# Where layer 3 gets its tiles from: first tile early, last tile from SBUF, next pair's first input made in layer 3

## Chip, cores and metric

The kernel runs on one core of a Trainium2 chip. The metric is device time in microseconds (us). The program computes four convolution layers on 16 images of 192 channels and 64x64 pixels in float32.

## What is computed

Every layer normalises its input in groups of six channels and adds its result to it. Layer 0 is a small per-channel network (a likelihood), layer 1 a convolution over five shifts, layer 2 a selective scan in four directions, layer 3 a depthwise convolution with a 1x1 mix, batch normalisation over all images and a clip. The reference, cut to layers 2 and 3:

```python
# layer 2: for each of 4 directions, over L = 4096 positions
dA = exp(d * A); h = dA * h + (d * u) * B_t; y = sum_n h * C_t      # 16 states n
x = x + ss2d(gn(x))
# layer 3
y = dw(x, w3) + dw(x, w5) + dw(x, wh) + dw(x, wv)     # 3x3, 5x5, 1x7, 7x1 depthwise
z = einsum('oc,bchw->bohw', pw, y)
zn = (z - mean(z)) * rsqrt(var(z) + 1e-5)             # over all images
x = x + clip(gamma * zn + beta, 0, 6)                 # input of dw is gn(x)
```

## The kernel before

Two images make a pair: 384 channels, which are three tiles (`NT`) of 128 partitions and `L` = 4096 columns. The eight pairs go one after the other. For the first pair, `front` (layers 0 and 1, the projections of layer 2) runs by itself; for each later pair it is woven, as a generator, into the `scans` of the pair before. So a pair is `scans(i)`, which also carries `front(i + 1)`, and then `layer3(i)`.

**scans.** For each tile j, direction k (in the order 1, 3, 0, 2) and chunk of 1024 columns there are 16 steps, one for each state n, 768 in all. A step is: `product` (DVE: pbt = du * B, out of PSUM), `scan` (DVE: the recurrence into h; ACT keeps the last column as `state`; POOL multiplies h by cb, the C row, and every fourth step starts a DMA that adds two h), `decay` (ACT: dA for a later step), `spread` (PE: B into PSUM), and `add_up` four steps late (PE: sums h over n into `ysum`; at n = 15 ACT copies it to X or Xt). `step_rest` makes delta and du for the next chunk out of `xn`, the normalised input tile, which `load_xn` and `norm_xn` bring in for each tile. When a tile is done, `finish(j)` adds Xt, transposed, to X in four pieces, takes statistics for layer 3 into `st3`, and stores X to `x3_d` in DRAM. For the last tile these adds are on DVE and nothing is left to run beside them.

**layer3.** It loads the three tiles of `x3_d` into `xp`, with three pixels of zero border, makes 21 diagonal 128x128 matrices on POOL (`diag`, a weight tap of seven for each tile), does the group norm on all three tiles' statistics (`group_norm`), and normalises each tile in place on DVE. Then for c in four pieces of 16 rows and for each tile j: eight taps go as ACT multiplies and POOL adds into `l3_g`; seven taps go as matmuls with `diag` into PSUM `l3_p`, to which PE adds `l3_g`; the last 14 taps go on DVE, one after the other, through `l3_p` into `l3_y`. After the three tiles PE mixes channels with `pw` into `zp`, ACT copies to z, DVE takes statistics, and SP stores z. At the end, when all pairs are done, z and x3 are read back, scaled, clipped and added.

**Order.** The tile framework lists the instructions of each engine in a fixed order at build time, by its own estimate of when each is ready. Instructions of `scans` are marked to stay in the order in which they were written; those of `layer3` are not, and may be put between them. A tile pool opened after others were closed takes their place in SBUF, in the order of opening, and waits for them. In `scans` the order is X, Xt, xn, dt, xc (16, 16, 16, 2 and 4 KB a partition), then bp, delta, du (20 KB in two buffers each), h (8 of 4 KB), dA (3), cb (4), then `front`'s pools; in `layer3` it is the small statistics (under 1 KB), xp (57 KB), pw and diag (14 KB), then l3_g, l3_m, l3_y and z (52 KB).

Line 64 in the profile is the helper through which all instructions of `scans` and a woven `front` go; line 319 is `normalise`.

Of the kernel before, what the change touches and what calls it, by code (L numbers as in the profile page):

```python
# [11 lines left out]
F32 = mybir.dt.float32  # L12
BF16 = mybir.dt.bfloat16
AF = mybir.ActivationFunctionType
ALU = mybir.AluOpType
# [7 lines left out]
P = 128  # L23
C = 192
NT = 3
HW = 64
L = HW * HW
BLOCKS = [(0, 0), (1, 0), (0, 1), (1, 1), (2, 1), (1, 2), (2, 2)]
INTO = [[(n, ji) for n, (ji, jo) in enumerate(BLOCKS) if jo == j] for j in range(NT)]
# [19 lines left out]
TAPS = [(3, 0), (3, 6), (0, 3), (6, 3)] + [(y, x) for y in range(1, 6) for x in range(1, 6)]  # L49
PE_TAPS = 7  # L50
# [54 lines left out]
def conv_preact_kernel(ctx: ExitStack, tc: tile.TileContext, a: dict):  # L105
    nc = tc.nc
    x_in = a["x"]
    out = a["out"]
    npair = x_in.shape[0]

    def row_tiles(ap):
        return ap.rearrange("(j p) l -> p j l", p=P)

    dram = ctx.enter_context(tc.tile_pool(name="dram", bufs=1, space=DRAM))
    x1_d = dram.tile([NT * P, L], F32, name="x1_d")
    x3_d = dram.tile([npair, NT * P, L], F32, name="x3_d")
    z_d = dram.tile([npair, NT * P, L], F32, name="z_d")
    zstat_d = dram.tile([npair, P, NT * 2], F32, name="zstat_d")
    wm_d = dram.tile([P, NG, P + GR], F32, name="wm_d")
    wt_d = dram.tile([GR, NG, 2 * P], F32, name="wt_d")  # L120

    const = ctx.enter_context(tc.tile_pool(name="const", bufs=1))
    ident = const.tile([P, P], F32, name="ident")
# [16 lines left out]
    def load(name, shape, pool=const):  # L140
        t = pool.tile(shape, F32, name="t_" + name, tag="t_" + name)
        nc.sync.dma_start(out=t, in_=a[name])
        return t
# [57 lines left out]
    with tc.tile_pool(name="prep", bufs=1) as prep, tc.tile_pool(  # L201
# [83 lines left out]
        for part, w in (  # L285
            (wc[:, :, 2:5, 2:5], w3x3),
            (wc[:, :, 3, :], w1x7),
            (wc[:, :, :, 3], w7x1),
        ):
            nc.vector.tensor_tensor(part, part, w, ALU.add)  # L290

# [14 lines left out]
            self.rstd = const.tile([P, NT], F32, name=f"rstd{n}")  # L308

    sets = [Made(n) for n in range(2)]  # L310

    def image(ap):
        return ap.rearrange("p (h w) -> p h w", w=HW)
# [4 lines left out]
    def normalise(eng, o, v, gm, rstd, j):  # L318
        eng.tensor_scalar(o, v, gm[:, j : j + 1], rstd[:, j : j + 1], ALU.subtract, ALU.mult)
# [14 lines left out]
                which = self._turn = (self._turn + 1) % self._many  # L334
            return self._pool.tile([P, 512], F32, name=name, tag=f"ps{which}")

    def group_norm(E, st, stat, ps, gm, rstd):

        mv = stat.tile([P, NT, 2], F32, name="mv", tag="mv")
        mean = stat.tile([P, NT], F32, name="mean", tag="mean")  # L340
        d2 = stat.tile([P, NT], F32, name="d2", tag="d2")
        half = stat.tile([P, NT], F32, name="half", tag="half")
        E.dve.memset(half, -0.5)
        for j in range(NT):
            E.dve.bn_aggr(mv[:, j, :], st[:, j, :, :].rearrange("p c s -> p (c s)"))
        E.dve.tensor_copy(mean, mv[:, :, 0])

        def mean_of(src):
            s = ps("gn_sum")
            for jo in range(NT):  # L350
                for n, (b, ji) in enumerate(INTO[jo]):
                    E.pe.matmul(
                        s[:, jo : jo + 1],
                        grp[:, b, :],
                        src[:, ji : ji + 1],
                        start=(n == 0),
                        stop=(n == len(INTO[jo]) - 1),
                    )
                yield
            return s[:, :NT]  # L360

        s = yield from mean_of(mean)
        E.dve.tensor_scalar(gm, s, 1.0 / 6.0, None, ALU.mult)
        E.dve.tensor_tensor(d2, mean, gm, ALU.subtract)
        E.dve.tensor_tensor(d2, d2, d2, ALU.mult)
        E.dve.tensor_tensor(d2, d2, mv[:, :, 1], ALU.add)
        s = yield from mean_of(d2)
        E.dve.tensor_scalar(d2, s, 1.0 / 6.0, 1e-5, ALU.mult, ALU.add)
        E.gps.tensor_tensor(rstd, d2, half, ALU.pow)
# [409 lines left out]
                yield  # L779


    def scans(i, o, st3, nxt):

        E = _Engines(tc, True)
        with ExitStack() as es:
# [11 lines left out]
            py = pool("l2_py", 1, space=PSUM)  # L797
            ps = Banks(pool("l2_ps", 1, space=PSUM), 2)

            X = one.tile([P, L], F32, name="X")  # L800
            Xt = one.tile([P, L], F32, name="Xt")

            todo = []
# [31 lines left out]

            def load_xn(j):
                if j < NT:
                    xns[j] = one.tile([P, L], F32, name="xn")
                    E.sp.dma_start(out=xns[j], in_=row_tiles(o.x2)[:, j, :])

            def norm_xn(j):
                if j < NT:
                    normalise(E.dve, xns[j], xns[j], o.gm, o.rstd, j)
# [119 lines left out]
            def finish(j):  # L963

                for c in range(4):
                    x = X[:, 1024 * c : 1024 * c + 1024]
                    eng = E.gps if j < NT - 1 else E.dve
                    eng.tensor_tensor(
                        image(x), image(x), columns(Xt)[:, 16 * c : 16 * c + 16, :], ALU.add
                    )  # L970
                    yield
                    yield

                    def stats(c=c):
                        for h in range(2 * c, 2 * c + 2):
                            E.dve.bn_stats(st3[:, j, h, :], X[:, 512 * h : 512 * h + 512])

                    E.later(stats)
                yield
                E.sp.dma_start(out=row_tiles(x3_d[i])[:, j, :], in_=X)  # L980

            load_xn(0)
            load_dt(0)
            load_bp(0)
            norm_xn(0)
            for _ in step_rest(0):
                pass
            load_dt(1)
# [6 lines left out]
            kind = None  # L995
            fin = iter(())
            gstep = iter(())
            for s in range(total):
                t, n = divmod(s, N)
                j, k, at, first = todo[t]  # L1000
# [18 lines left out]
                    norm_xn(j + 1)  # L1019
                if n > 4:  # L1020
                    next(fin, None)

                if n == 3:
                    add_up(s - LATE)
# [21 lines left out]
            for g in (finish(NT - 1), fr):  # L1046
                for _ in g:
                    E.between()
            E.between()

    def layer3(i, st3):
        E = _Engines(tc, False)
        with tc.tile_pool(name="l3s", bufs=1) as stat, tc.tile_pool(name="l3x", bufs=1) as xk, tc.tile_pool(
            name="l3w", bufs=1
        ) as w_, tc.tile_pool(name="l3", bufs=2) as wk, tc.tile_pool(
            name="l3_pt", bufs=2, space=PSUM
        ) as pt, tc.tile_pool(name="l3_pz", bufs=4, space=PSUM) as pz:
            S = HW + 6
            xp = xk.tile([P, NT, S, S], F32, name="xp")
            inside = slice(3, 3 + HW)  # L1060
            for j in range(NT):
                nc.sync.dma_start(
                    out=xp[:, j, inside, inside], in_=image(row_tiles(x3_d[i])[:, j, :])
                )
            pw = load("pw", [P, len(BLOCKS), P], w_)
            diag = w_.tile([P, NT, PE_TAPS, P], F32, name="diag")
            for edge in (slice(0, 3), slice(3 + HW, S)):
                nc.gpsimd.memset(xp[:, :, edge, :], 0.0)
                for j in range(NT):
                    nc.gpsimd.memset(xp[:, j, inside, edge], 0.0)  # L1070
            for j in range(NT):
                for t, (ty, tx) in enumerate(TAPS[:PE_TAPS]):
                    nc.gpsimd.tensor_scalar(
                        diag[:, j, t, :], ident, wc[:, j, ty, tx : tx + 1], None, ALU.mult
                    )
            gm = stat.tile([P, NT], F32, name="gm")
            rstd = stat.tile([P, NT], F32, name="rstd")
            banks = lambda name: pz.tile([P, 512], F32, name=name, tag="ps")
            for _ in group_norm(E, st3, stat, banks, gm, rstd):
                pass  # L1080
            for j in range(NT):
                v = xp[:, j, inside, inside]
                normalise(nc.vector, v, v, gm, rstd, j)
            zst = stat.tile([P, NT, 8, 6], F32, name="zst")
            def window(j, c, rows, tap):
                return xp[:, j, c + tap[0] : c + tap[0] + rows, tap[1] : tap[1] + HW]

            def factor(j, tap):
                return wc[:, j, tap[0], tap[1] : tap[1] + 1]

            own = PE_TAPS + GP_TAPS
            for c in range(4):
                ys = []
                for j in range(NT):

# [58 lines left out]
            for j in range(NT):  # L1154
                nc.vector.bn_aggr(zmv[:, j, :], zst[:, j, :, :].rearrange("p c s -> p (c s)"))
            nc.sync.dma_start(out=zstat_d[i], in_=zmv.rearrange("p j s -> p (j s)"))

    def pair(i, q, more):

        with tc.tile_pool(name="st3", bufs=1) as p3:  # L1160
            st3 = p3.tile([P, NT, 8, 6], F32, name="st3")
            scans(i, sets[q], st3, None if more is None else (more, sets[1 - q]))
            layer3(i, st3)

    with tc.tile_pool(name="f_ps", bufs=1, space=PSUM) as ps:
        for _ in front(0, sets[0], _Engines(tc, False), Banks(ps, 8), True):
            pass
    for i in range(npair):
        pair(i, i % 2, i + 1 if i + 1 < npair else None)


    with tc.tile_pool(name="fin", bufs=1) as fin, tc.tile_pool(
# [164 lines left out]
```

## Time and profile before

| | |
|---|---|
| median of three runs | 28266.48 us (28245.82 to 28275.6) |
| profiled execution | 28295.17 us, span of its instructions 28293.1 us |
| busy share | DVE 86%, PE 83%, POOL 73%, ACT 57% |
| DVE, costliest | scans of h 10811.0 + 3509.0 us, products 7441.2 us, taps of layer 3 1589.7 us |
| POOL, costliest | h*cb 14853.6 us, adds of layer 3 1614.3 us |
| first pair: first product, last scan ended | 1212.9, 4207.9 us |
| first pair: layer 3, first tap to last statistics | 4254.3 to 4555.1 us |
| second pair: first product | 4572.6 us |

The page of a profile counts, for each engine, the time in which it executed something; matmuls overlap one another, so PE's share says least. A share over the whole span is a mean over stages with different limits. The stage between the end of one pair's scans and the start of the next pair's is therefore read from the timeline, instruction by instruction, with, in brackets, how long the engine stood idle before and what ended that.

### The profile page before, as it was taken

The page shows a single profiled execution, that of the slowest core. Times are in us where ns is not written, and L with a number is a line of the kernel's source. Part 1 is how long each engine was busy: PE and PEld are TensorE (multiplying, and loading weights), DVE is VectorE, ACT ScalarE, POOL GpSimd, SP SyncE. Part 2 cuts the span into 40 slices and gives each one's busy share as a digit, 9 for nine tenths or more (in the row PEclk, how much of TensorE's full clock was granted, in tenths as well). Part 3 has the DMA queues.
Part 4 walks back from the last instruction along what each step waited for, and adds up shares of the span by engine and source line. Part 5 has one row for each costly group of instructions (what it writes and reads, how often), then busy time and mean ns, then how long its engine had stood idle before and what let it go on. Part 6 is the DMA issues. An engine that isn't in the chain of part 4 may idle for free. (4 is left out here: it accounts for less than half of the span.)

```text
span 28293.1 us, 208020 instructions
## 1 busy us (share of the span) xinstructions
PE 23483.5 (83%) x57140; PEld 9639.0 (34%) x57140; DVE 24223.9 (86%) x15397; ACT 16092.7 (57%) x23037; POOL 20787.2 (73%) x10440
## 2 busy tenths in 40 slices
PE   8799977999689986999779997799968998766663
PEld 4343323333233332333324332333323333222221
DVE  0399988998889988999989998899988998899994
ACT  7377445774467643775547744577446764344433
POOL 2388876887768876788768887688777887677772
PEclk9899988999899998999889998899989999888886
DMA  4479864897568973888748986489756897367765
GB/s 101 133 219 220 213 199 139 220 218 211 159 180 222 218 215 116 219 218 220 210 125 218 219 215 198 136 220 219 213 162 176 220 219 212 115 189 191 191 182 232
DMA packets 2008001, 5447.99 MB, mean 193 GB/s; under 512 B 550393, under 2 KB 550617, under 8 KB 1989425
## 3 DMA queue, kind: packets, MB, share of 16 engines
q1 hardware_dynamic: 1782192, 4578.95, 56.1%
q0 software_dynamic: 221184, 805.40, 14.9%
q10 hardware_dynamic: 3456, 50.33, 0.4%
q8 instruction: 455, 7.45, 0.1%
q14 instruction: 714, 5.84, 0.1%
HBM read 3896.19 MB, written 329.51 MB: 149 GB/s over the span
## 5 line engine op out<-in xcount | busy, mean ns | idle before, releaser
L64 POOL TENSOR_TENSOR h<-h,cb 128x1024 f32<-128x1024 f32 x6144 | 14853.6, 2465 | 4470.5 <-ACT state L64 3854.4
L64 DVE TENSOR_TENSOR_SCAN h<-dA,state,pbt 128x1024 f32<-128x1024 f32 x4608 | 10811.0, 2346 | 659.1 <-ACT dA L64 97.5
L64 PE MATMUL ysum<-h,ident 128*128 128x512 f32 x18432 | 9459.7, 638 | 191.6 <-DMA h<-h 144.7
L64 DVE TENSOR_TENSOR pbt<-du,pbt 128x1024 f32<-128x1024 f32 x6144 | 7441.2, 1211 | 852.4 <-PE pbt L64 812.1
L64 ACT ACTIVATE dA<-delta,t_alog 128x1024 f32<-128x1024 f32 x6144 | 7034.8, 1146 | 6.6
L64 PEld LDWEIGHTS ysum<-h,ident 128*128 128x128 f32 x18432 | 3780.8, 206 | 4474.2 <-issue 3926.6
L64 ACT COPY state<-h 128x1 f32<-128x1 f32 x6144 | 1141.0, 186 | 6533.9 <-DVE h L64 6508.4
L64 PE MATMUL pbt<-bp,pick 96*128 96x512 bf16 x8192 | 2729.3, 418 | 1942.8 <-DVE h L64 1931.8
L64 DVE TENSOR_TENSOR_SCAN h<-dA,pbt 128x1024 f32<-128x1024 f32 x1536 | 3509.0, 2285 | 181.5 <-DVE pbt L64 30.8
L64 PE MATMUL p<-t,wts 96*128 96x512 f32 x5376 | 2783.4, 618 | 164.0 <-ACT t L64 163.0
L64 PE MATMUL p<-m,wms 128*96 128x512 f32 (+1 forms) x5376 | 2720.3, 609 | 12.0 <-ACT lu L64 12.0
L64 ACT ACTIVATE t<-p,bias 96x512 f32<-96x512 f32 x2688 | 1803.6, 678 | 1162.8 <-PE p L64 1151.6
L64 PEld LDWEIGHTS <-pick 96*128 96x128 bf16 x8192 | 715.6, 102 | 4759.1 <-DVE h L64 2927.7
L1104 POOL TENSOR_TENSOR l_g<-l_g,l_m 128x1024 f32<-128x1024 f32 x672 | 1614.3, 2404 | 454.4 <-ACT l_g L1100 349.0
L64 PE MATMUL l_p<-l_xp,w1s 128*128 128x512 f32 x3920 | 1868.7, 609 | 0.0
L1127 DVE SCALAR_TENSOR_TENSOR l_p<-xp,wc,l_p 128x1024 f32<-128x1024 f32 x1248 | 1589.7, 1287 | 266.6 <-PE l_p L1121 235.8
L64 PE MATMUL pbt<-bp,pick_mix 96*128 96x512 bf16 x4096 | 1302.3, 401 | 569.8 <-DVE h L64 564.9
L64 POOL DMA_DIRECT2D h<-h x1536 | 1354.3, 882 | 495.1 <-POOL h L64 429.8
L1109 PE MATMUL l_p<-xp,diag 128*128 128x512 f32 x2688 | 1293.2, 641 | 331.9 <-DVE l_y L1127 281.2
L64 PEld LDWEIGHTS p<-t,wts 96*128 96x128 f32 x5376 | 1032.6, 195 | 1335.9 <-issue 903.1
L64 ACT ACT_TABLE_LOAD x1104 | 1416.4, 1283 | 19.3
L64 POOL TENSOR_TENSOR du<-delta,xn 128x1024 f32<-128x1024 f32 x384 | 1039.1, 2706 | 452.4 <-ACT delta L64 452.4
(219 smaller groups left out, 17710.1 us busy)
## 6 DMA issues: line engine op xcount, KB each, us to landing
cb<-cp_d SPq DMA_DIRECT2D x2048, 512.0 KB
cb<-c_d SPq DMA_DIRECT2D x2048, 512.0 KB
h<-h POOLq DMA_DIRECT2D x1536, 512.0 KB, 7.0
cb<-cp_d SPq DMA_DIRECT2D x2048, 256.0 KB
cb<-c_d SPq DMA_DIRECT2D x2048, 256.0 KB
m<-l_xn SPq DMA_DIRECT2D x3072, 128.0 KB
bp<-bp_d SPq DMA_DIRECT2D x384, 192.0 KB
f0x<-in_x SPq DMA_DIRECT2D x96, 512.0 KB
```

Source lines behind the costliest of these rows:

```text
L64: return self._tc.keep_in_program_order(call(*args, **kw))
L1104: nc.gpsimd.tensor_tensor(g, g, m, ALU.add)
L1109: nc.tensor.matmul(ps[:, cs], diag[:, j, t, :], window(j, 16 * c + 8 * h, 8, tap), start=(t == 0), stop=False,)
L1127: nc.vector.scalar_tensor_tensor(image(y if tap is TAPS[-1] else ps), window(j, 16 * c, 16, tap), factor(j, tap), image(ps), ALU.mult, ALU ...
```

## The change

Five things are changed together.

1. The 21 diagonal matrices are made once, in the preparation, and stored to `diag_d`; each `layer3` loads them.
2. `X` and `xn` move into a pool `over` that stays open. The last tile's sum isn't read back from `x3_d`: layer 3 normalises it out of X, and its store stands behind the loads of layer 3.
3. `group_norm` can be done for some tiles. A first one over tiles 0 and 1 (`gn0`) runs in the last 11 steps of the scans; it gives the mean and the scale of tile 0, whose groups end in tile 1. Layer 3 normalises tile 0 with these, in four pieces, before the group norm of all three.
4. `xp` becomes three tiles, in a pool opened last in layer 3, placed in the order 2, 0, 1.
5. The next pair's first `xn` is loaded and normalised in `layer3`, written at c = 2; the first pair's after the first `front`. `scans` begins without it.

```diff
+    diag_d = dram.tile([P, NT, PE_TAPS, P], F32, name="diag_d")
...
+        for j in range(NT):
+            diag = prep.tile([P, PE_TAPS, P], F32, name="diag", tag="diag", bufs=2)
+            for t, (ty, tx) in enumerate(TAPS[:PE_TAPS]):
+                nc.gpsimd.tensor_scalar(
+                    diag[:, t, :], ident, wc[:, j, ty, tx : tx + 1], None, ALU.mult
+                )
+            nc.sync.dma_start(out=diag_d[:, j, :, :], in_=diag)
...
+    over = ctx.enter_context(tc.tile_pool(name="over", bufs=1))
...
-    def group_norm(E, st, stat, ps, gm, rstd):
+    def group_norm(E, st, stat, ps, gm, rstd, tiles=range(NT)):
...
+    def first_xn(o):
+
+        xn = over.tile([P, L], F32, name="xn")
+        nc.sync.dma_start(out=xn, in_=row_tiles(o.x2)[:, 0, :])
+        return xn
...
-            X = one.tile([P, L], F32, name="X")
...
-                E.sp.dma_start(out=row_tiles(x3_d[i])[:, j, :], in_=X)
-
-            load_xn(0)
+                if j < NT - 1:
+                    E.sp.dma_start(out=row_tiles(x3_d[i])[:, j, :], in_=X)
+
+            xns[0] = xn0
             load_dt(0)
             load_bp(0)
-            norm_xn(0)
...
+            gn0 = group_norm(E, st3, p3, ps, gm0, rstd0, range(2))
...
+                if t == T - 1 and n > 4:
+                    next(gn0, None)
...
+            xps = {j: xk.tile([P, S, S], F32, name=f"xp{j}") for j in (2, 0, 1)}
+            for j in range(NT - 1):
+                nc.sync.dma_start(
+                    out=xps[j][:, inside, inside], in_=image(row_tiles(x3_d[i])[:, j, :])
+                )
+            diag = w_.tile([P, NT, PE_TAPS, P], F32, name="diag")
+            nc.sync.dma_start(out=diag, in_=diag_d)
+            pw = load("pw", [P, len(BLOCKS), P], w_)
+            nc.sync.dma_start(out=row_tiles(x3_d[i])[:, NT - 1, :], in_=X)
...
+            for r in range(0, HW, 16):
+                v = xps[0][:, 3 + r : 19 + r, inside]
+                normalise(nc.vector, v, v, gm0, rstd0, 0)
             for _ in group_norm(E, st3, stat, banks, gm, rstd):
                 pass
-            for j in range(NT):
-                v = xp[:, j, inside, inside]
-                normalise(nc.vector, v, v, gm, rstd, j)
+            v = xps[1][:, inside, inside]
+            normalise(nc.vector, v, v, gm, rstd, 1)
+            normalise(nc.vector, xps[2][:, inside, inside], image(X), gm, rstd, 2)
...
             for c in range(4):
+                if c == 2 and o_next is not None:
+                    xn = first_xn(o_next)
+                    normalise(nc.vector, xn, xn, o_next.gm, o_next.rstd, 0)
```

More of the change, by code (lines that the diff above doesn't have):

```diff
@@ L335, in __call__ @@
             return self._pool.tile([P, 512], F32, name=name, tag=f"ps{which}")
-    def group_norm(E, st, stat, ps, gm, rstd):
+    def group_norm(E, st, stat, ps, gm, rstd, tiles=range(NT)):
+        m = len(tiles)
         mv = stat.tile([P, NT, 2], F32, name="mv", tag="mv")
@@ L343, in group_norm @@
         E.dve.memset(half, -0.5)
-        for j in range(NT):
+        for j in tiles:
             E.dve.bn_aggr(mv[:, j, :], st[:, j, :, :].rearrange("p c s -> p (c s)"))
+        mean, d2, half, mv = mean[:, :m], d2[:, :m], half[:, :m], mv[:, :m, :]
+        gm, rstd = gm[:, :m], rstd[:, :m]
         E.dve.tensor_copy(mean, mv[:, :, 0])
@@ L349, in mean_of @@
             s = ps("gn_sum")
-            for jo in range(NT):
-                for n, (b, ji) in enumerate(INTO[jo]):
+            for jo in tiles:
+                into = [x for x in INTO[jo] if x[1] in tiles]
+                for n, (b, ji) in enumerate(into):
                     E.pe.matmul(
@@ L356, in mean_of @@
                         start=(n == 0),
-                        stop=(n == len(INTO[jo]) - 1),
+                        stop=(n == len(into) - 1),
                     )
                 yield
-            return s[:, :NT]
+            return s[:, :m]
         s = yield from mean_of(mean)
@@ L779, in split, with scans @@
                 yield
-    def scans(i, o, st3, nxt):
+    def first_xn(o):
+        xn = over.tile([P, L], F32, name="xn")
+        nc.sync.dma_start(out=xn, in_=row_tiles(o.x2)[:, 0, :])
+        return xn
+    def scans(i, o, p3, st3, X, xn0, nxt):
         E = _Engines(tc, True)
@@ L837, in load_xn @@
                 if j < NT:
-                    xns[j] = one.tile([P, L], F32, name="xn")
+                    xns[j] = over.tile([P, L], F32, name="xn")
                     E.sp.dma_start(out=xns[j], in_=row_tiles(o.x2)[:, j, :])
@@ L997, in scans @@
             gstep = iter(())
+            gm0 = p3.tile([P, NT], F32, name="gm0")
+            rstd0 = p3.tile([P, NT], F32, name="rstd0")
+            gn0 = group_norm(E, st3, p3, ps, gm0, rstd0, range(2))
             for s in range(total):
@@ L1049, in scans, with layer3 @@
             E.between()
-    def layer3(i, st3):
+            for _ in gn0:
+                pass
+            return gm0, rstd0
+    def layer3(i, st3, X, gm0, rstd0, o_next):
         E = _Engines(tc, False)
-        with tc.tile_pool(name="l3s", bufs=1) as stat, tc.tile_pool(name="l3x", bufs=1) as xk, tc.tile_pool(
-            name="l3w", bufs=1
-        ) as w_, tc.tile_pool(name="l3", bufs=2) as wk, tc.tile_pool(
+        with tc.tile_pool(name="l3s", bufs=1) as stat, tc.tile_pool(name="l3w", bufs=1) as w_, tc.tile_pool(
+            name="l3", bufs=2
+        ) as wk, tc.tile_pool(name="l3x", bufs=1) as xk, tc.tile_pool(
             name="l3_pt", bufs=2, space=PSUM
@@ L1058, in layer3 @@
             S = HW + 6
-            xp = xk.tile([P, NT, S, S], F32, name="xp")
             inside = slice(3, 3 + HW)
-            for j in range(NT):
[L1062 to L1075, printed above, removed]
+            xps = {j: xk.tile([P, S, S], F32, name=f"xp{j}") for j in (2, 0, 1)}
[7 more added lines that the diff above has]
+            nc.sync.dma_start(out=row_tiles(x3_d[i])[:, NT - 1, :], in_=X)
+            for j in range(NT):
+                for edge in (slice(0, 3), slice(3 + HW, S)):
+                    nc.gpsimd.memset(xps[j][:, edge, :], 0.0)
+                    nc.gpsimd.memset(xps[j][:, inside, edge], 0.0)
             gm = stat.tile([P, NT], F32, name="gm")
@@ L1078, in layer3 @@
             banks = lambda name: pz.tile([P, 512], F32, name=name, tag="ps")
+            for r in range(0, HW, 16):
+                v = xps[0][:, 3 + r : 19 + r, inside]
+                normalise(nc.vector, v, v, gm0, rstd0, 0)
             for _ in group_norm(E, st3, stat, banks, gm, rstd):
                 pass
-            for j in range(NT):
-                v = xp[:, j, inside, inside]
-                normalise(nc.vector, v, v, gm, rstd, j)
+            v = xps[1][:, inside, inside]
+            normalise(nc.vector, v, v, gm, rstd, 1)
+            normalise(nc.vector, xps[2][:, inside, inside], image(X), gm, rstd, 2)
             zst = stat.tile([P, NT, 8, 6], F32, name="zst")
             def window(j, c, rows, tap):
-                return xp[:, j, c + tap[0] : c + tap[0] + rows, tap[1] : tap[1] + HW]
+                return xps[j][:, c + tap[0] : c + tap[0] + rows, tap[1] : tap[1] + HW]
             def factor(j, tap):
@@ L1091, in layer3 @@
             own = PE_TAPS + GP_TAPS
+            xn = None
             for c in range(4):
+                if c == 2 and o_next is not None:
+                    xn = first_xn(o_next)
+                    normalise(nc.vector, xn, xn, o_next.gm, o_next.rstd, 0)
                 ys = []
@@ L1156, in layer3, with pair @@
             nc.sync.dma_start(out=zstat_d[i], in_=zmv.rearrange("p j s -> p (j s)"))
-    def pair(i, q, more):
+            return xn
+    def pair(i, q, more, xn):
         with tc.tile_pool(name="st3", bufs=1) as p3:
             st3 = p3.tile([P, NT, 8, 6], F32, name="st3")
-            scans(i, sets[q], st3, None if more is None else (more, sets[1 - q]))
-            layer3(i, st3)
+            X = over.tile([P, L], F32, name="X")
+            nxt = None if more is None else (more, sets[1 - q])
+            first = scans(i, sets[q], p3, st3, X, xn, nxt)
+            return layer3(i, st3, X, *first, None if more is None else sets[1 - q])
     with tc.tile_pool(name="f_ps", bufs=1, space=PSUM) as ps:
@@ L1167, in conv_preact_kernel @@
             pass
+    xn = first_xn(sets[0])
+    normalise(nc.vector, xn, xn, sets[0].gm, sets[0].rstd, 0)
     for i in range(npair):
-        pair(i, i % 2, i + 1 if i + 1 < npair else None)
+        xn = pair(i, i % 2, i + 1 if i + 1 < npair else None, xn)
     with tc.tile_pool(name="fin", bufs=1) as fin, tc.tile_pool(
```

## The prediction

> **What bounds the kernel now.** I read the page first (parts 1 and 5), then a table by windows around the end of the first pair's scans, then the timeline of the same place, and last the start of the second pair. Part 1 gives DVE 86% of the span, and the windows say where the rest is: (columns: busy us and instructions of PE, PEld, DVE, ACT, POOL; clock; DMA share; GB/s)
>
> ```profile
> 4100.00:4207.87 107.87, 78.30 (x166) 29.68 (x165) 103.93 (x60) 40.61 (x63) 80.87 (x41) 0.82 0.61 177
> 4207.87:4254.34 46.47, 13.90 (x42) 8.77 (x41) 16.55 (x23) 1.21 (x3) 16.98 (x30) 0.61 0.44 120
> 4254.34:4279.31 24.97, 18.39 (x37) 6.94 (x37) 4.33 (x2) 14.65 (x13) 22.09 (x9) 0.77 0.62 133
> 4279.31:4555.13 275.82, 220.43 (x508) 88.39 (x508) 233.66 (x196) 110.45 (x108) 179.69 (x76) 0.90 0.05 22
> 4555.13:4572.61 17.48, 3.99 (x8) 1.06 (x8) 2.42 (x2) 4.22 (x5) 2.85 (x1) 0.52 0.59 208
> ```
>
> In the last scan steps DVE is busy 103.93 of 107.87 us: it is the bound there. From its last scan (call this e, 4207.87) to layer 3's first tap (4254.34) lie 46.5 us in which DVE works 16.6; the first tap on DVE comes 25.0 later (e+71.4), and from the end of layer 3 to the next pair's first product pass another 17.5 with DVE busy 2.4. Layer 3 itself (275.8 us from DVE's first tap) is DVE-bound at 85%. What fills the first gap:
>
> ```profile
> 4206.95 8.71 POOL L1073 TENSOR_SCALAR diag<-ident,wc 128x128 f32<-128x128 f32 x15
> 4215.63 2.33 POOL L64 TENSOR_TENSOR h<-h,cb 128x1024 f32<-128x1024 f32 x1
> ...
> 4218.02 3.64 PE L64 MATMUL ysum<-h,ident 128*128 128x512 f32 x4 [5.82 <-POOL h L64]
> ...
> 4221.70 1.01 ACT L64 COPY X<-ysum 128x1024 f32<-128x1024 f32 x1 [13.61 <-PE ysum L64]
> 4222.74 3.70 DVE L64 TENSOR_TENSOR X<-X,Xt 128x1024 f32<-128x1024 f32 x2 [14.88 <-ACT X L64]
> ...
> 4232.51 0.32 SPq L64 DMA_DIRECT2D x_d<-X  x1
> 4238.81 20.56 SPq L1062 DMA_DIRECT2D xp<-x_d  x3
> ...
> 4248.23 0.89 POOL L369 TENSOR_TENSOR rstd<-d,half 128x3 f32<-128x3 f32 x1 [6.82 <-DVE d L368]
> 4251.84 2.41 DVE L319 TENSOR_SCALAR xp<-xp,gm,rstd 128x4096 f32<-128x4096 f32 x1 [3.70 <-DMA xp<-x_d]
> 4254.31 14.70 PE L1109 MATMUL l_p<-xp,diag 128*128 128x512 f32 x28 [6.36 <-DVE xp L319]
> 4254.34 1.15 ACT L1100 ACTIVATE l_g<-xp,wc 128x1024 f32<-128x1024 f32 x1 [31.63 <-DVE xp L319]
> ```
>
> The reader should see one chain: 15 diagonal matrices on POOL stand ahead of the last h*cb, which comes 7.5 us late (it could start at 4208.1, when the state copy is done); then the last sums on PE, the copy to X, four adds with statistics on DVE (12.1 us, to e+26.9), the store of X, its landing at 4238.81, and only then three tile loads, of which the first is used 13.0 us later. The second gap:
>
> ```profile
> 4555.16 0.32 SPq L1156 DMA_DIRECT2D zstat_d<-zmv  x1
> 4556.98 0.32 SPq L64 DMA_DIRECT2D xn<-x_d  x1
> 4557.35 0.80 SPq L64 DMA_DIRECT2D dt<-dtp_d  x2
> ...
> 4566.09 2.41 DVE L64 TENSOR_SCALAR xn<-xn,gm,rstd 128x4096 f32<-128x4096 f32 x1 [10.97 <-DMA xn<-x_d]
> 4566.28 2.16 PE L64 MATMUL v<-dt,t_dtw 12*128 12x512 f32 x4 [12.91 <-DMA dt<-dtp_d]
> ...
> 4569.72 2.85 POOL L64 TENSOR_TENSOR du<-delta,xn 128x1024 f32<-128x1024 f32 x1 [62.14 <-ACT delta L64]
> 4572.61 1.23 DVE L64 TENSOR_TENSOR pbt<-du,pbt 128x1024 f32<-128x1024 f32 x1 [4.10 <-DMA cb<-cp_d]
> ```
>
> The 2 MB load of xn is issued ahead of the small dt loads; all land at 4566, and v, delta and du follow. All eight ends of scans in the trace have these gaps within 1 us (46.0 to 47.2, and 16.7 to 18.2 for the seven starts), so each edit counts 8 or 7 times.
>
> **What the Trainium skill says.** "DMA: Bandwidth & Descriptors", section "Queues, rings and completion order": each DMA engine takes descriptors in ring order. The trace agrees: of the three xp loads issued together at 4238.81, tile 0 is used at 4251.84 and tile 1 at 4261.72, so one tile costs 13.0 us alone and about 10 more behind another. "SBUF — State Buffer", section "SBUF: two separate sides": VectorE and GpSimd hold their shared port pair exclusively, one blocking the other for a whole instruction. It agrees: the normalise of 128x4096 takes 2.41 us with POOL idle and 4.33 or 3.94 with POOL adding. "TensorE: Matmul & The Clock Gate", section "What's actually happening": an idle PE restarts at half clock. It agrees: 28 diagonal matmuls take 14.70 us after the gap and 12.43 warm.
>
> **The change, part by part** (relative to e).
>
> *Diagonals to DRAM.* 21 POOL operations (594 ns each) go from each pair. The last h*cb then runs e+0.2 to e+2.6; PE is free of the sums before it at 4212.2 (e+4.3), so the last four matmuls end at e+6.2 instead of e+13.8, the copy to X at e+7.3 instead of e+14.8, the finish at e+19.4 instead of e+26.9. In return a 1.38 MB load per pair, and once 21 operations and three stores in the preparation, beside its 60 us; POOL's softplus chain is near, so I allow 2 us there, 0 to 5.
>
> *What layer 3's first tile waits for.* A pool waits for every reader of the pools it lies on, not only for the tile below: the xn load at 4556.98 waited 1.4 us for the statistics' store, though 32 KB from it. By the tile sizes in the code, the new l3s and l3w (diag, pw) lie under Xt's pool, the work tiles l3 under that pool and h's, and the xps tiles under h, dA and cb. So the xps loads are free when PE has read the last h, e+6.2, whatever their order; diag, pw and the first l_g are free when the fourth add has read Xt, about e+17. Tile 0 lands at e+6.3+13.0 = e+19.3, just as the finish leaves DVE (e+19.4); its first two quarters (0.6 us each) are done at e+20.6, with gm0 and rstd0 long there. ACT's first tap is at e+20.7 instead of e+46.5: 25.8 earlier.
>
> *What is late next: diag.* On the ring it stands behind tiles 0 and 1: tile 1 lands at e+29.3, diag 1.38 MB later; at the 210 GB/s of the xp loads (2.1 MB in 10 us) 6.6 us, so e+36. PE's cold 28 matmuls end at e+50.7, l_g's (ready at 20.7+21.2 = e+41.9) add 2 to 3.7, and DVE's first tap is at e+53.5 instead of e+71.4: 18 earlier. Behind it the first two tiles lose a normalise (3.9 us, now done in the wait) and a wait for l_g (1.5): 41 us become 35, and the third tile starts 23 earlier. From there the stage is DVE-bound as before. I take 23 per pair: 184. Bounds: 15, if the normalises or the group statistics stand badly in DVE's queue (before the last adds they hold up Xt and with it diag), to 30, if DVE finishes tile 0 before tile 1 instead of interleaving them as now, which frees PSUM for tile 2. The X store goes behind diag and pw on SP, and with it whatever SP has next, the first z store some 80 us later: free. The edge memsets (12 of about 0.3 us on POOL) fill e+6 to e+10, before tile 0 lands; without that cover they would cost their 3.6 us.
>
> *gn0 in the last scan steps.* One group norm more on DVE, where nothing covers it: from part 5 style rows memset 0.06, two aggregates 0.66, copy 1.93, four small operations 0.13+1.07+0.16+0.86, one 0.15, 5.0 us, and up to 0.7 twice for PE's sums: 5.5. POOL's pow (0.9) lies in its slack. Loss 44 (40 to 50). Queued behind its waits are the product and scan of the next step.
>
> *The next pair's input.* Without xn ahead, dt (issued 4557.35) needs a landing like the statistics' store (1.8 us): about 4559.6, v 2.16 to 4561.8, delta 1.11, du 2.85: product at 4565.8 instead of 4572.6. 6.8 each for seven pairs, 6.3 for the first pair (same chain): 54 (45 to 62). Its 2 MB load becomes free 24 steps before e, when the last du is made, and SP may issue it there (DMA share 0.61, so 10 us are absorbed) or in layer 3 (0.05). The normalise is no longer bare (2.41) but on DVE somewhere: nothing in the gap after e, 3.9 to 4.3 in layer 3, 4.6 on average (8.4 at most) in the scans. I take 3.5, seven times: 25 (0 to 60).
>
> *End.* The final tiles lie elsewhere, so the last statistics' store may go ahead of two zl and rl loads it now waits behind (18.2 us): 5 (0 to 15).
>
> Sum: 184 - 44 + 54 - 25 + 5 - 2 = 172 off 28295.17, the profiled execution (span 28293.1 and 2.1 around it), 28123. The median of the runs is 28.7 lower, 28266.48; the same 172 gives 28094, rounded to 28095.
>
> **Rivals.** (a) The head start is mostly eaten in front of DVE: PE's taps, which wait for diag, stand in PE's queue ahead of the group sums, or DVE's normalises wait ahead of the last adds. For: the order is fixed by a planner that already set diagonals ahead of the last h*cb. Against: most of these waits end before e+36 anyway. At 10 per pair: 80-44+54-25+3 = 68, 28198. (b) Better: no interleaving, xn's normalise in the gap: 30x8-44+54+15-2 = 263, 28003. (c) No change: the head start is lost in layer 3, as POOL's adds (201.8 us of the stage) or the z sums bound its first third: 20-44+54-25 = 5, 28260. (d) Slower: xn's normalise stands in DVE's queue ahead of the finish, and its load is third on the ring behind tiles 0 and 1, landing 32 us after issue as xp's third does (4238.8 to about 4271); DVE stands for 32+4.6 at each of seven ends: 256 instead of 25 gives 172+25-256 = -59, 28325. It decides from a wait of 28 us per end. Against: the load is free long before e.
>
> **How the numbers follow.** Forecast 0.70, (a) 0.12, (b) 0.08, (c) 0.05, (d) 0.05. Own range of the forecast: 15x8-50+45-60 = 55 to 30x8-40+62-0+15 = 277 off at the extremes; leaving the tails out and reaching to (a) and (b): 28000 to 28200. About 0.2% (57 us) can be told from no change. Faster by more: 0.85 (nearly all of the forecast, b and most of a); within: 0.10 (c, the rest of a and of the forecast); slower: 0.05.
>
> **What would show it.** In the new trace: last h*cb within 3 us of the last scan; copy to X at e+7; first ACT tap near e+21 and first diagonal matmul near e+36, the latter waiting for a DMA; first DVE tap near e+53; 11 us instead of 17.5 to the next product; scans some 5 us longer. If the first DVE tap comes before e+45, diag didn't wait; if scans grow by more than 10 us, xn's load or normalise sits in them. Wrong altogether if layer 3 grows from its 300.8 us (first ACT tap to the end) by more than the 26 it starts earlier.

## The result

The changed kernel takes 28184.44 us (median of ten runs, 28169.6 to 28207.6); the kernel before took 28264.15 beside it (28245.82 to 28276.97). The ratio is 0.9973, interval [0.9963, 0.9983]: 80 us less. The whole interval lies below 1, so the changed kernel is faster, by about 0.3%. The time lies inside the stated range, but the forecast was 172 less. The profiled execution after has a span of 28176.2 us.

First the windows of the profile after (columns as in the prediction), for the first pair and cut at the same events as before: last scan, ScalarE's (ACT's) first tap, VectorE's (DVE's) first tap, end of layer 3, next product.

```profile
4213.43:4245.57 32.14, 12.55 (x44) 8.68 (x42) 17.16 (x25) 1.21 (x3) 5.92 (x14) 0.68 0.78 182
4245.57:4270.46 24.89, 17.74 (x37) 6.61 (x37) 4.33 (x4) 14.67 (x13) 22.06 (x9) 0.77 0.22 92
4270.46:4548.50 278.04, 221.34 (x508) 88.34 (x508) 230.25 (x195) 110.45 (x108) 177.94 (x76) 0.89 0.07 27
4548.50:4558.96 10.46, 3.90 (x8) 0.97 (x8) 0.07 (x1) 4.22 (x5) 2.82 (x1) 0.54 0.41 137
```

Beside the windows of before, the first has become 14.3 us shorter (46.47) and the last 7.0 (17.48). The second has hardly changed (24.97), and the third is 2.2 us longer, although the normalise of the third tile, which stood in it, is now done before it. So layer 3 starts earlier, but gives some of it back inside. The timeline of the same place, after:

```profile
4213.73 2.35 POOL L64 TENSOR_TENSOR h<-h,cb 128x1024 f32<-128x1024 f32 x1 [1.22 <-ACT state L64]
...
4219.73 9.84 SPq L1092 DMA_DIRECT2D xp<-x_d  x2
4230.52 8.65 SPq L1096 DMA_DIRECT2D diag<-diag_d  x1
...
4232.79 0.38 DVE L358 BATCH_NORM_AGGREGATE mv<-st 128x2 f32<-128x48 f32 x1
...
4241.11 0.16 DVE L384 TENSOR_SCALAR d<-gn_sum 128x3 f32<-128x3 f32 x1 [3.24 <-PE gn_sum L368]
4242.27 2.41 DVE L330 TENSOR_SCALAR xp<-X,gm,rstd 128x4096 f32<-128x4096 f32 x1 [1.00 <-POOL rstd L385]
4244.60 5.30 DVE L330 TENSOR_SCALAR xp<-xp,gm,rstd 128x1024 f32<-128x1024 f32 x5
...
4245.57 1.15 ACT L1134 ACTIVATE l_g<-xp,wc 128x1024 f32<-128x1024 f32 x1 [24.86 <-DVE xp L330]
...
4309.27 2.61 DVE L1161 SCALAR_TENSOR_TENSOR l_p<-xp,wc,l_p 128x1024 f32<-128x1024 f32 x2 [1.71 <-PE l_p L1155]
4324.85 0.69 DVE L1183 BATCH_NORM_STATS2 zst<-z 128x6 f32<-128x512 f32 x1 [12.97 <-ACT z L1182]
```

The last h*cb ends at e+2.6 and tile loads are issued at e+6.3, both as forecast. But the row of five pieces (the four of tile 0, and tile 1) stands behind the whole group norm, from 4232.79 to 4241.11, and behind tile 2's normalise, which waits for that group norm: tile 0 has its own numbers, and doesn't get to use them. The last row is the second surprise. VectorE begins the third tile at 4309.27, does two of its 14 taps, and then stands 12.97 us for the first z. The same two rows in the timeline of before:

```profile
4325.35 2.61 DVE L1127 SCALAR_TENSOR_TENSOR l_p<-xp,wc,l_p 128x1024 f32<-128x1024 f32 x2 [5.12 <-PE l_p L1121]
4330.98 0.69 DVE L1149 BATCH_NORM_STATS2 zst<-z 128x6 f32<-128x512 f32 x1 [3.02 <-ACT z L1148]
```

Relative to e, the third tile is 21.6 us earlier (e+117.5 before, e+95.8 after), the first z statistics only 11.7 (e+123.1, e+111.4), and the end of layer 3 12.1 (e+347.3, e+335.1).

The start of the second pair, after:

```profile
4548.60 0.32 SPq L1190 DMA_DIRECT2D zstat_d<-zmv  x1
4550.42 0.72 SPq L64 DMA_DIRECT2D dt<-dtp_d  x2
...
4556.14 2.85 POOL L64 TENSOR_TENSOR du<-delta,xn 128x1024 f32<-128x1024 f32 x1 [54.90 <-ACT delta L64]
4559.03 1.23 DVE L64 TENSOR_TENSOR pbt<-du,pbt 128x1024 f32<-128x1024 f32 x1 [10.46 <-DMA cb<-cp_d]
```

No load of xn and no normalise is left here; the two are found inside the scans, at 4126.38 and 4140.42 (3.77 us on VectorE), 73 us before e.

### The profile page after: what moved, and what is told of

It is laid out like the page before. It is cut to its first block, busy times and chain, and to the rows that moved or that the text cites. A ratio compares the mean times of both kernels' runs of the same rounds, so it can differ in the third digit from the quotient of the medians.

```text
span 28176.2 us, 208219 instructions
## 1 busy us (share of the span) xinstructions
PE 23454.3 (83%) x57268; PEld 9632.3 (34%) x57268; DVE 24245.7 (86%) x15493; ACT 16097.9 (57%) x23037; POOL 20716.6 (74%) x10333
```

## The experiments

All times are medians; ratios are to runs of the kernel before on the same chip. e1 to e4, e5 to e8 and e9 ran on three chips, on which the kernel before took 28273, 28258 and 28282 us, so between these groups the ratios are to be compared. The table was worked out from the traces: each entry is the median over the eight pairs, relative to e (the next product: seven pairs, after the end of layer 3). "Not adding" is the time between GpSimd's (POOL's) first and 28th add of layer 3 in which it did no add.

| kernel | us, ratio | ACT first tap | DVE first tap | not adding | 28th add ends | first z stat. | layer 3 ends | next product |
|---|---|---|---|---|---|---|---|---|
| before | 28264 | 46.5 | 71.5 | 1.9 | 120.4 | 123.1 | 347.3 | 17.6 |
| after | 28184, 0.9973 [0.9963, 0.9983] | 31.7 | 56.6 | 6.5 | 108.3 | 111.0 | 334.6 | 10.5 |
| e1 tile 0 first | 28155, 0.9959 [0.9947, 0.9972] | 20.0 | 51.7 | 12.4 | 104.4 | 107.2 | 331.2 | 10.7 |
| e2 no early group norm | 28157, 0.9960 [0.9947, 0.9972] | 31.6 | 56.5 | 6.5 | 108.1 | 110.9 | 336.6 | 10.3 |
| e3 before + diagonals loaded | 28206, 0.9978 [0.9969, 0.9987] | 38.5 | 63.6 | 1.9 | 112.5 | 115.2 | 339.9 | 16.9 |
| e4 before + early xn | 28196, 0.9972 [0.9962, 0.9983] | 38.6 | 63.5 | 1.9 | 112.4 | 115.2 | 339.8 | 13.0 |
| e5 before + diagonals in order | 28202, 0.9979 [0.9970, 0.9987] | 38.8 | 63.8 | 1.9 | 112.7 | 115.5 | 340.3 | 17.7 |
| e6 interleaved | 28149, 0.9959 [0.9946, 0.9971] | 21.4 | 51.1 | 11.0 | 104.4 | 107.1 | 331.2 | 10.4 |
| e7 diagonals' load earlier | 28108, 0.9946 [0.9933, 0.9958] | 21.4 | 52.4 | 6.4 | 99.7 | 102.4 | 327.5 | 10.3 |
| e8 preparation in order | 28175 (one run) | 31.9 | 56.8 | 6.5 | 108.5 | 111.2 | 334.8 | 10.5 |
| e9 power later | 28100, 0.9934 [0.9921, 0.9948] | 21.2 | 47.1 | 2.6 | 95.8 | 98.6 | 323.7 | 10.4 |

One regularity runs through all 88 layer 3s in it. The first z statistics come 2.7 us after the end of the 28th add, and the end of layer 3 comes 222 to 226 us after these statistics, whatever VectorE did until then. The first tap on VectorE doesn't rank the kernels: e7 has it later than e6 and ends 3.7 us earlier. GpSimd's adds before, and then after:

```profile
4256.67 71.59 POOL L1104 TENSOR_TENSOR l_g<-l_g,l_m 128x1024 f32<-128x1024 f32 x28 [7.55 <-ACT l_m L1100]
```

```profile
4247.85 35.77 POOL L1138 TENSOR_TENSOR l_g<-l_g,l_m 128x1024 f32<-128x1024 f32 x14 [5.62 <-ACT l_m L1134]
4285.92 16.98 POOL L1138 TENSOR_TENSOR l_g<-l_g,l_m 128x1024 f32<-128x1024 f32 x7 [2.30 <-ACT l_g L1134]
4305.20 16.93 POOL L1138 TENSOR_TENSOR l_g<-l_g,l_m 128x1024 f32<-128x1024 f32 x7 [2.30 <-ACT l_g L1134]
```

A piece of three tiles has only 21 adds (seven a tile), so the last seven here belong to the next piece, and the first z needs none of them. It waits for them all the same, through the order on ACT. PE and ACT, after:

```profile
4309.15 7.13 PE L1175 MATMUL zp<-l_y,t_pw 128*128 128x512 f32 x16
...
4322.16 1.15 ACT L1134 ACTIVATE l_m<-xp,wc 128x1024 f32<-128x1024 f32 x1 [1.26 <-POOL l_g L1138]
4323.22 1.13 ACT L1134 ACTIVATE l_g<-xp,wc 128x1024 f32<-128x1024 f32 x1
4324.26 0.56 ACT L1182 COPY z<-zp 128x512 f32<-128x512 f32 x1
```

PE mixes the channels from 4309.15 on, but ACT's first copy to z comes at 4324.26, behind multiplies of the next piece, which go at the pace of the adds because `l_m` has three buffers. VectorE's statistics of this z in turn stand ahead of 12 of the third tile's 14 taps. The order is the same in the kernel before, where the wait was 3.02 us. No run here moves the copy or the statistics, so what that would gain is open.

**e1: VectorE's order.**

```diff
+            O = _Engines(tc, True)
             for r in range(0, HW, 16):
-                normalise(nc.vector, v, v, gm0, rstd0, 0)
-            for _ in group_norm(E, st3, stat, banks, gm, rstd):
+                normalise(O.dve, v, v, gm0, rstd0, 0)
+            for _ in group_norm(O, st3, stat, banks, gm, rstd):
```

`O` keeps the written order among the instructions that go through it; tiles 1 and 2 are normalised through `O.dve` too.

> The changed kernel with one thing changed: on VectorE tile 0's four normalising pieces come straight after the finish's last statistics, and the whole group norm with the normalising of tiles 1 and 2 behind them. Theory A (the order on VectorE cost the head start, and ScalarE's and GpSimd's tap chain sets layer 3's length): ScalarE's first tap at about e+21 instead of e+32.1, first third's y of tile 0 at about e+70, end of layer 3 about 11 us earlier in each pair, 8 x 11 = 88 us less than the changed kernel: about 28096. Rival B (TensorE's diagonal weights, which land at about e+34, or VectorE are the bound from here on): ScalarE's first tap at e+21 too, but the end of layer 3 only 0 to 5 us earlier, 0 to 40 less. Rival C (the later normalising of tiles 1 and 2 takes the place): no change.

The first tap on ACT moved to e+20.0, near the e+20.7 of the forecast. The end moved by 3.4 us a pair: the size of rival B, not of theory A. But neither the diagonals nor VectorE explain the table's "not adding", which rose from 6.5 to 12.4: GpSimd began 12 us earlier and lost half of that among its first adds. The cause is seen best in e6.

**e2: no early group norm.** `gn0` is taken out; tile 0's four pieces use `gm` and `rstd` and follow the group norm.

> The changed kernel without the separate group norm of tiles 0 and 1 in the last scan steps; tile 0 is normalised with the numbers of the whole group norm. Theory A (in the order that the changed kernel has on VectorE, the early group norm buys nothing): ScalarE's first tap stays at e+31 to e+33, layer 3 keeps its length, and the scan stage is about 5.3 us shorter in each pair: 8 x 5.3 = 42 us less than the changed kernel, about 28142. Rival B (tile 0 needs the early numbers): the first tap is 5 us or more later and the time is equal to that of the changed kernel or above it.

The first tap stayed at e+31.6 (31.5 to 32.5): in the order that the change has on VectorE, the early group norm buys nothing. Against the changed kernel the time is 27 us less by the medians and 37 by the ratios, whose intervals overlap, where 42 was expected. What the early norm costs is cleanest in the last pair, whose scans carry no `front`: 2792.3 us without it, 2798.3 to 2798.7 in the six kernels with it, so 6.2 us. Layer 3 here ends 2 us later than in the changed kernel with the same first z; the cause is open.

**e3, e4, e5: parts of the change alone.** e3 takes only the diagonals through DRAM, e4 only the early xn with the pool `over`. e5 takes neither; it marks GpSimd's 21 diagonals and the zero borders (edges) to keep the written order, with the edges written behind the diagonals:

```diff
+        kept = _InOrder(tc, nc.gpsimd)
...
-                    nc.gpsimd.tensor_scalar(
+                    kept.tensor_scalar(
```

> The kernel before with one part of the change: the diagonal weights are made once, kept in DRAM and loaded in each layer 3, so that GpSimd has no such work at the end of the scans. Theory A (GpSimd's diagonals delayed the last h*cb by 7.5 us, and everything up to layer 3's first tap follows it): last h*cb at e+2.6, end of layer 3 7 to 8 us earlier in each pair, less 8 us lost in the preparation, so 48 to 56 us less than before. Rival B (what follows waits for something else, the store and reload of the last tile): last h*cb at e+2.6, first tap at most 2 us earlier, time within 20 us of before.

> The kernel before with one part of the change: the next pair's first input is loaded and normalised in layer 3. Theory A (its load and wait at the head of the scans cost 7 us in each pair but the first, and its normalising is hidden): next product 10.5 us after layer 3 instead of 17.5, 7 x 7 + about 6 for the first pair = 50 to 55 us less than before. Rival B (its normalising takes VectorE's time at full length): 3.8 x 7 = 27 us of it given back, 22 to 28 less.

> The kernel before; GpSimd's diagonals and edges keep the order of the program, so the 21 diagonals follow the last h*cb instead of standing ahead of it. Nothing is loaded from DRAM. Theory A (what the diagonals cost was their place ahead of the last h*cb): last h*cb at e+2.6, ScalarE's first tap about 7.5 us earlier, 8 x 7.5 = 60 us less than before, about 28213, and no loss in the preparation. Rival B (they then hold the edges or the diagonals back until after tile 0 is normalised): last h*cb at e+2.6 but first tap at e+44 or later, at most 20 us less than before.

All three have the last h*cb at e+2.6 and the first tap at about e+38.6. e3 and e5 come near their theories A (62 and 59 us less by the ratios). e4 gained 79, more than either of its theories had: it too moved the diagonals behind the last h*cb, without a line about them: the tile framework ordered GpSimd's work otherwise, presumably because xn lies elsewhere in SBUF. So the parts aren't additive; three different edits collect the same 7 us. GpSimd in e5:

```profile
4218.22 2.34 POOL L64 TENSOR_TENSOR h<-h,cb 128x1024 f32<-128x1024 f32 x1 [1.22 <-ACT state L64]
4220.55 18.71 POOL L64 TENSOR_SCALAR diag<-ident,wc 128x128 f32<-128x128 f32 x21
```

The diagonals now take 18.71 us beside VectorE's adds, 0.89 each instead of 0.58, and nobody waits for them: the tiles, stored and read back, come later still. In e4 the product chain came 13.0 us after layer 3, not 10.5, because a load for the next `front` stood ahead of dt on SP; at the last start, which has no `front`, it came after 10.8.

**e6: the start of the group norm ahead of tile 0.**

```diff
+            g3 = group_norm(O, st3, stat, banks, gm, rstd)
+            next(g3)
             for r in range(0, HW, 16):
                 normalise(O.dve, v, v, gm0, rstd0, 0)
-            for _ in group_norm(O, st3, stat, banks, gm, rstd):
+            for _ in g3:
```

`next(g3)` writes the variances, the means and the first of TensorE's sums.

> As the run with tile 0's pieces first, but the group norm's first two steps on VectorE (variances and means) stand ahead of the pieces, so that TensorE's group sums are out of the way of its diagonal taps. Theory A (TensorE's group sums at e+25 to e+32 held its taps): TensorE's first tap moves from e+32 to the landing of the diagonals, at about e+29 to e+34, VectorE's first tap 0 to 3 us earlier than e+51 to e+52.6, 0 to 24 us less than that run's 28155. Rival B (the landing of the diagonals at about e+34 holds them): TensorE's first tap stays at e+32 to e+35 and the time within 10 us of 28155.

TensorE's (PE's) first tap stayed at e+31.8 to 34.4 and the time within 6 us of e1, with the same ratio: rival B, as to TensorE. GpSimd's timeline in e6 shows what really holds the stage:

```profile
4257.49 2.35 POOL L1141 TENSOR_TENSOR l_g<-l_g,l_m 128x1024 f32<-128x1024 f32 x1 [14.96 <-ACT l_m L1137]
4263.54 0.87 POOL L64 TENSOR_TENSOR rstd<-d,half 128x3 f32<-128x3 f32 x1 [3.70 <-DVE d L64]
4264.40 35.27 POOL L1141 TENSOR_TENSOR l_g<-l_g,l_m 128x1024 f32<-128x1024 f32 x13
```

After one add the queue holds the power (`rstd`) of the group norm of all tiles, whose input VectorE has only 3.70 us later; the second add, whose inputs are there, stands behind it. The Trainium skill says this of the queues: "PSUM — Partial Sum Buffer", section "Engine vs sequencer instructions", calls those of ScalarE, VectorE and GpSimd strictly first in, first out. This trace agrees: the second add starts at 4264.40, when the power ends, 4.56 us after the first. Starting tile 0 early on ACT is of no use while GpSimd's queue holds, behind the first add, an instruction that belongs to the other tiles.

**e7: the diagonals' load between tiles 0 and 1**, and, in the preparation, GpSimd's diagonals kept behind the softplus work (e8 has this second edit alone, on the changed kernel).

```diff
+            diag = w_.tile([P, NT, PE_TAPS, P], F32, name="diag")
             for j in range(NT - 1):
+                if j == 1:
+                    nc.sync.dma_start(out=diag, in_=diag_d)
                 nc.sync.dma_start(
...
-            diag = w_.tile([P, NT, PE_TAPS, P], F32, name="diag")
-            nc.sync.dma_start(out=diag, in_=diag_d)
```

> As the interleaved run, with the diagonals' load issued between those of tiles 0 and 1, and GpSimd's diagonals in the preparation kept behind the softplus work. Theory A (TensorE's first tap waits for the diagonals, VectorE's for TensorE): TensorE's first tap at about e+27, VectorE's at about e+46, end of layer 3 about e+326, 5 us earlier in each pair than the run with tile 0's pieces first, and the first product 8 us earlier, at 1207: 28155 - 40 - 8 = about 28107. Rival B (ScalarE's and GpSimd's chain of eight taps holds VectorE): VectorE's first tap not earlier than e+50, only the 8 us of the start gained, about 28147.

> The changed kernel; GpSimd's diagonals in the preparation are kept behind the softplus work. Theory A (their place among the softplus operations delayed the first weights' store): first product at about 1207 instead of 1215.3, all else as in the changed kernel, 8 us less. Rival B (the diagonals' store on SyncE's queue is what delays it): first product at 1213 to 1216.

28108 is what theory A had named, but not by its way. TensorE's first tap did come to e+29.3, and VectorE's was at e+52.4, as rival B had it. The 3.7 us a pair came from elsewhere: the tile framework, presumably with other ready times, put ACT's first tap of each tile ahead of the next multiply, so that two gaps of 2.30 us among the adds are gone (11.0 to 6.4). In e6 the second of these rows is

```profile
4301.97 16.95 POOL L1141 TENSOR_TENSOR l_g<-l_g,l_m 128x1024 f32<-128x1024 f32 x7 [2.30 <-ACT l_g L1137]
```

and in e7 27 adds run without it, in 69.10 us. The other gain is the start. In the changed kernel GpSimd's diagonals stand among the softplus operations:

```profile
24.10 7.33 POOL L295 TENSOR_SCALAR diag<-ident,wc 128x128 f32<-128x128 f32 x10
31.41 0.58 POOL L193 TENSOR_TENSOR sp_e<-sp_e,sp_w 96x192 f32<-96x192 f32 x1
```

and the store of the weights `wm_d` goes out at 66.98. With the order kept (e8) the diagonals begin at 28.74, behind the last softplus operation, the store goes out at 58.92, and the first product comes at 1205.8 instead of 1215.3: theory A of e8.

**e9: the power behind the third add.** On top of e7, the rest of the group norm and the normalises of tiles 1 and 2 are written after the third add of tile 0:

```diff
-                            nc.gpsimd.tensor_tensor(g, g, m, ALU.add)
+                            (O.gps if c + j == 0 else nc.gpsimd).tensor_tensor(g, g, m, ALU.add)
+                        if c + j == 0 and tap is TAPS[PE_TAPS + 3]:
+                            for _ in g3:
+                                pass
...
```

> As the run with the diagonals' load between tiles 0 and 1; only the end of the group norm (its last sums, GpSimd's power, the normalising of tiles 1 and 2) is put behind GpSimd's third add of tile 0 instead of behind the first. Theory A (GpSimd's power waits on GpSimd's queue for the group norm until about e+30, and the adds behind it with it; GpSimd's chain of adds sets the first third): no wait of 3.7 us ahead of the power, GpSimd's adds of tile 0 without a gap from about e+24, VectorE's first tap at about e+47 instead of e+52.5, end of layer 3 about 4 to 5 us earlier in each pair, 8 x 4.5 = 36 us less: about 28072. Rival B (TensorE's taps from e+29 to e+45 and the sums behind them hold VectorE all the same): VectorE's first tap at e+49 or later and at most 1 us gained in each pair, about 28100 to 28108.

GpSimd in e9, and VectorE's first tap:

```profile
4232.08 7.21 POOL L64 TENSOR_TENSOR l_g<-l_g,l_m 128x1024 f32<-128x1024 f32 x3 [14.93 <-ACT l_m L1135]
4239.26 0.88 POOL L64 TENSOR_TENSOR rstd<-d,half 128x3 f32<-128x3 f32 x1
4240.12 13.48 POOL L64 TENSOR_TENSOR l_g<-l_g,l_m 128x1024 f32<-128x1024 f32 x4
...
4255.64 13.21 DVE L1168 SCALAR_TENSOR_TENSOR l_p<-xp,wc,l_p 128x1024 f32<-128x1024 f32 x10 [6.67 <-PE l_p L1162]
```

The power no longer waits, VectorE's first tap is at e+47.1, and layer 3 ends 3.1 to 4.1 us earlier than in e7 in every pair: theory A, in its mechanism. Of the 29 us that this makes in eight pairs, the ratio shows 34 and the bare medians, from two chips, 9; 28100 by itself would fit rival B. The intervals of e7 and e9 overlap, so the step is shown by the boundaries in the trace and not by the times. e9 is the fastest of all: 0.9934 of the kernel before, where the change has 0.9973.

## Why the prediction was wrong

The forecast was 184 - 44 + 54 - 25 + 5 - 2 = 172 us off. By its terms:

- **The head start, 184 (23 a pair): measured 101 (12.6 a pair). This is the step that failed.** It has two halves. First, "ACT's first tap is at e+20.7 instead of e+46.5: 25.8 earlier" was built on tile 0's pieces following the finish; on VectorE they stand behind the group norm and tile 2's normalise, and the tap is 14.8 earlier, at e+31.7. e1 and e6 show that the arrival of data allowed e+20 to e+21. Second, "from there the stage is DVE-bound as before" is false for the first third. In the first pair the third tile did start 21.6 earlier, near the 23 of the text, and VectorE then waited 12.97 us instead of 3.02 for z. What sets the first third is the chain of ACT's multiplies and GpSimd's 28 adds, behind which the copy to z stands: the tap is 14.8 earlier, 4.6 us more lie between the adds, which themselves take 1.9 less, and so the first z is 12 earlier. Both halves are needed: with the first mended (e1) the end moved by 3.4; with ACT's order and GpSimd's queue mended too (e7, e9) it is 23.5 us earlier than before. That this is the predicted 23 is in part luck, since VectorE's first tap is then at e+47.1 and not at the e+53.5 on which the 23 was built.
- **What is late next: diag, e+36, DVE's first tap e+53.5.** TensorE's first tap, waiting for diag, came at e+31.8 to 34.4 (e6), so the landing was 2 to 4 us earlier than placed; but e7 took that wait away and VectorE's tap came no earlier.
- **gn0, -44:** 6.2 us in the last pair, against 5.5 forecast; 50 for eight, if the other pairs lose as much, which isn't shown. Their seven scans together took 21002 to 21051 us in the six kernels with gn0 and the early xn, 21009 in both with the early xn alone (e2, e4), and 20971 to 20994 in the three with neither.
- **The next product, 54:** seven times 7.1 us (17.6 to 10.5) is 50. The first pair's 6.3 was right (e4, without diagonals in the preparation: 1206.6 instead of 1212.9).
- **xn's normalise, -25:** it went into the scans, at 3.8 to 4.2 us, 27 for seven; the 21009 above, against 20971 to 20994, fits that.
- **The end, 5:** the stretch after the last layer 3 took 4.5 us less. The loads and the store stand there in the order that was forecast, but e5, in the old order, took 3.6 less too, so the cause isn't shown.
- **The preparation, -2, bound 5: outside its bound.** It cost 9.5 (e8 against the changed kernel; 9.6 in e3 against before). "Beside its 60 us" counted GpSimd's free time, and not that ten diagonals could be set ahead of a short chain for which everything waits.

With these sizes the sum is 101 - 50 + 50 + 6 - 27 + 5 - 10 = 75, against 80 measured; as gn0's 50 is extrapolated, the nearness proves little. The two profiled executions are 117 apart, since that of before lay 31 us above the median of its runs and that of after 6 below. Rival (a), at 28198, came nearest in size. Its place, VectorE's queue, was right, with another instruction in the way; the mechanism inside layer 3 was that of rival (c).

## What to carry over

When work is started earlier, follow every engine's queue of the stage and not the bound engine's alone: an early tile is worth only what the slowest chain behind it (here ACT's multiplies and GpSimd's adds) gains, and an instruction of the later tiles, set between its links, takes the gain away. Ask also whether the result waited for needs the whole chain, or only stands behind it in a queue, as the first z does here. Check what an engine waits for at the end of the part that you shorten, since a wait of 3 us there may hide a second chain 3 us behind the first. Compare kernels by boundaries inside the trace, of which the first z statistics repeat within 1.3 us over a kernel's eight pairs here, before comparing whole times.

## What the hardware showed beside that

- A 128x3 operation on VectorE takes 0.16 us alone and took 2.27 when it fell beside a GpSimd add of 2.35 (e6, the square in the group norm); normalises of 128x4096 took 4.43 beside adds and 2.41 without.
- The issue of a load isn't always short: with two 2 MB loads of 256-byte rows queued ahead, that of the diagonals held SP for 8.65 us, and in e7, where it stood second, 0.33; there the small load of pw behind three others held SP for 11.67.
- The scans of a pair with a woven `front` took 2996.9 to 3019.1 us within one execution (e8), though each pair runs the same instructions; those of the last pair, without a `front`, agree within 0.4 us over the six kernels with the early group norm. The cause is open.
